# Neighbourhood attention by bands of 8 columns: a change to layer 0 of a four-layer hybrid kernel

## The chip, the core and the metric
The kernel runs on one core of a Trainium2 chip. The core has a matrix engine (PE in the profile, its weight loads PEld), a vector engine (DVE), a scalar engine that evaluates functions (ACT), a general one (POOL) and a queue that issues transfers (SP). Each engine executes its instructions in the order of the program; between engines there are semaphores. Data lie in an on-chip memory of 128 partitions, matrix products arrive in PSUM. The metric is the time of one execution in microseconds; less is better.

## The reference
Four layers run over an image tensor of shape (4, 56, 56, 128). The change touches layer 0 alone, attention of each pixel over a 7 x 7 neighbourhood, with 4 heads of 32 channels and a bias that depends on the relative position:
```python
qkv = (x @ w_qkv + b_qkv).reshape(B_, H_, W_, 3, nh, hd)
si = jnp.clip(jnp.arange(H_) - nb, 0, H_ - k)      # k = 7, nb = 3
sj = jnp.clip(jnp.arange(W_) - nb, 0, W_ - k)
...
attn = jnp.einsum('bnijd,bnipjqd->bnijpq', q, k_win) + bias[None]
attn = softmax over the 49 keys of a window
out = jnp.einsum('bnijpq,bnipjqd->bnijd', attn, v_win)
...
x = x + _L0_conv_ref(_gn(x), ...)                  # _gn: group norm over the image
```
At the border the window is shifted inwards, so that it always has 49 keys. Layers 1 to 3 (a selective scan, two attentions, two mixtures of experts) follow on the result.

## The kernel before
**Tiling.** An image has 3136 pixels. A *chunk* is 8 rows of 56 pixels (`SEQ` = 8, `CH` = 448), 7 chunks an image, 28 in all. Queries are columns of a matrix product, keys are its partitions. A *tile of keys* is 2 whole rows, 112 keys. A chunk's 8 query rows need 14 rows of keys, so up to 8 such tiles; each tile is met by the query rows whose windows touch it. `key_tiles` packs these (tile, query rows) pairs into *units* of exactly 448 query columns: 4 units a chunk, 112 in all, most of two pairs. Every unit computes all 112 x 448 scores, those outside a pixel's window too; these are later multiplied by zero.

**One unit.** `scores(i)` (L486): for each pair and head a matmul of 32 channels x 112 keys against the query columns; the four heads lie in the four row groups of the array and write to four PSUM banks. There are two such pairs of banks for halves of a unit, so the next unit's scores wait for the exps of this one. `weights(i)`: two exps on ACT (L496), then a product with exp(bias) (L502), three heads on DVE, one on POOL. `sums(i)` (L517): for each pair and head a matmul with the values (tile `o`) and one with ones (tile `d`, the denominator).

**One chunk.** `queries`, `keys`, `values` (L449, L457, L464) project the normed image; `finish` has four steps: `copied` (ACT takes `o` and `d` out of PSUM, POOL adds a bias into X, L533), `divided` twice (DVE: reciprocal L537 and product L538 on halves), `projected` (PE L543 and a DVE addition into X, L546). All small products of this kind and the transposes share a PSUM tile `m` with two buffers.

**Order.** The order on PE, ACT, DVE and POOL is written out by hand. In turn i of the main loop come the scores of unit i+1, the sums of unit i-1, the weights of unit i+1, and then the steps listed in `at[i]`: with four units a chunk, the queries of chunk k+1 at the first turn of chunk k, keys and values of chunk k+2 at the second and third, the steps of `finish` at turns 0 to 3 of the next chunk, 12 steps of the next image's norm one every one and a half turns (seven of them transpose a chunk, take its statistics on DVE and copy it on ACT), and 42 small steps that form layer 1's weights on DVE, one every second turn.

**Tables.** exp(bias) depends on the row offset, the key's column and the query's column. `make()` in `bias_tables` multiplies the bias by a constant table of 14 x 56 x 56, takes exps, writes them to DRAM (`dtab`, 7 transfers, L303) and reads them back into tables for inner rows and both edges (16 transfers, L311 and L318).

Of the kernel before, what the change touches and what calls it, by code (L numbers as in the profile page):

```python
# [10 lines left out]
F32 = mybir.dt.float32  # L11
AF = mybir.ActivationFunctionType
ALU = mybir.AluOpType
# [19 lines left out]
NEG = -1.0e30  # L33

# [32 lines left out]
def host_constants():  # L67

    j = np.arange(HW)
    start = np.clip(j - NB, 0, HW - KW)  # L70
    kj = j[:, None]
    inside = (kj >= start[None, :]) & (kj < start[None, :] + KW)
    toep = np.zeros((1 + KR, HW, HW), np.float32)
    toep[KR] = np.where(inside, 0.0, NEG)
    for d in range(KR):
        toep[d] = inside & (kj - j[None, :] + KW - 1 == d)
    turn = np.zeros((NH, KR, KR, NH), np.float32)
    for h in range(NH):
        for r in range(KR):
            turn[h, r, KR - 1 - r, h] = 1.0  # L80
# [24 lines left out]
    for i in range(B):  # L105
# [8 lines left out]
        "k_toep": toep.reshape(1 + KR, HW * HW),  # L114
        "k_turn": turn.reshape(NH * KR, KR * NH),
# [6 lines left out]
class Hybrid:  # L122
# [61 lines left out]
    def group_norm(self, b, pool, group):  # L184
# [11 lines left out]

        def turn(c, psum):
            g.ps = psum()
            for k in range(TC):
                nc.tensor.transpose(  # L200
                    g.ps[:, k * TP : (k + 1) * TP], self.X[b][:, TC * c + k, :],
                    self.ident[:TP, :TP],
                )
# [61 lines left out]
        g.place, g.turn, g.stats, g.raw = place, turn, stats, raw  # L265
        g.groups, g.normed, g.scaled = groups, normed, scaled
# [5 lines left out]
    def bias_tables(self, pool, tmp, big, dr, m):  # L272

        nc, a = self.nc, self.a
        inner = self.t(pool, [TP, 9, NH, HW], "e_inner")
        edge = [self.t(pool, [TP, 4, NB, NH, HW], f"e_edge{k}") for k in range(2)]
        nc.gpsimd.memset(inner, 0.0)
        for e in edge:  # L280
            nc.gpsimd.memset(e, 0.0)
        rpb = self.load(tmp, [NH * KR, KR], "rpb", a["L0_conv_rpb"].rearrange("h r d -> (h r) d"))
        order = self.load(tmp, [NH * KR, KR * NH], "rpb_turn", a["k_turn"])
        toep = self.t(big, [P, HW, HW], "xnT").rearrange("p k j -> p (k j)")[: 1 + KR]
        nc.sync.dma_start(out=toep, in_=a["k_toep"])
        rT = self.t(tmp, [1 + KR, KR * NH], "rpbT")
        nc.vector.memset(rT, 1.0)

        def make():

            ps = m()
            nc.tensor.matmul(ps[:KR, : KR * NH], rpb, order, start=True, stop=True)
            nc.vector.tensor_copy(rT[:KR], ps[:KR, : KR * NH])
            dtab = dr.tile([HW, KR, NH, HW], F32, name="dtab")
            rows = CH // HW
            for c in range(NCH):
                tab = self.t(tmp, [KR * NH, CH], "tab", bufs=4)
                ps = m()[: KR * NH]
                nc.tensor.matmul(
                    ps[:, :CH], rT, toep[:, c * CH : (c + 1) * CH], start=True, stop=True  # L300
                )
                nc.scalar.activation(tab, ps[:, :CH], AF.Exp)
                nc.sync.dma_start(  # L303
                    out=dtab[c * rows : (c + 1) * rows].rearrange("k r h j -> (r h) k j"),
                    in_=tab.rearrange("p (k j) -> p k j", j=HW),
                )
            for at, (q0, r0) in enumerate(((0, 0), (HW - NB, HW - KW))):
                for r in range(r0, r0 + KW):
                    t, r2 = r // 2, r % 2
                    first = KW - 1 - r + q0  # L310
                    nc.sync.dma_start(  # L311
                        out=edge[at][r2 * HW : (r2 + 1) * HW, t - r0 // 2],
                        in_=dtab[:, first : first + NB],
                    )
                if at:
                    continue
                for r2 in range(2):
                    nc.sync.dma_start(  # L318
                        out=inner[r2 * HW : (r2 + 1) * HW, 1 + r2 : 1 + r2 + KW],
                        in_=dtab[:, NB : NB + KW],  # L320
                    )

        return (inner, edge), make

    @staticmethod
    def window(i):
        return min(max(i - NB, 0), HW - KW)

    def key_tiles(self, c):


        rows = range(SEQ * c, SEQ * (c + 1))
        parts = []
        for t in range(NT):
            mine = [i for i in rows if self.window(i) <= 2 * t + 1 and self.window(i) + KW > 2 * t]
            if mine:
                parts.append((t, mine[0] - rows[0], mine[-1] + 1 - rows[0]))
        parts.sort(key=lambda x: x[1] - x[2])
        groups = []
        for p in parts:  # L340
            n = p[2] - p[1]
            for g in groups:

                if all(x[2] <= p[1] or p[2] <= x[1] for x in g):
                    g.append(p)
                    break
            else:
                groups.append([p])
        once = lambda g: sorted(i for _, q0, q1 in g for i in range(q0, q1)) == list(range(SEQ))
        return sorted(groups, key=lambda g: not once(g))  # L350

    def bias_slices(self, tables, c, part):

        inner, edge = tables
        t, q0, q1 = part
        out = []
        i = q0
        while i < q1:
            row = SEQ * c + i
            end = NB if row < NB else HW - NB if row < HW - NB else HW  # L360
            n = min(q1, end - SEQ * c) - i
            if row < NB:
                tab = edge[0][:, t, row : row + n]
            elif row >= HW - NB:
                tab = edge[1][:, t - (HW - KW) // 2, row - (HW - NB) : row - (HW - NB) + n]
            else:
                k = row - 2 * t + NB + 1
                tab = inner[:, k : k + n]
            out.append((i - q0, n, tab))
            i += n  # L370
        return out

    def layer0(self, wp1):
# [5 lines left out]
        with ExitStack() as ctx:  # L379
            wp = ctx.enter_context(tc.tile_pool(name="l0_w", bufs=1))  # L380
            dr = ctx.enter_context(tc.tile_pool(name="b_dram", bufs=1, space=DRAM))
# [9 lines left out]
            tables, make_tables = self.bias_tables(wp, wp, big, dr, m)  # L391
# [6 lines left out]
            make_tables()  # L398
# [11 lines left out]
            groups = {c: self.key_tiles(c) for c in range(NCH)}  # L410
            units = [(k, g) for k, (b, c) in enumerate(chunks) for g in range(len(groups[c]))]
            xn, q, kT, v, sc, es, out = {}, {}, {}, {}, {}, {}, {}

            def norm_steps(b):
                g = self.group_norm(b, big, group)

                def chunk(c):
                    if c == 0:
                        g.place(big)
                    g.turn(c, m)  # L420
                    g.stats(c)
                    g.raw(c)

                def hand_over():
                    g.normed(range(4, NCH))
                    xn[b] = g.xn.rearrange("p i j -> p (i j)")
# [16 lines left out]
            def chunk_of(k):  # L443
                b, c = chunks[k]
                return xn[b][:, c * CH : (c + 1) * CH]

            def queries(k):
                ps = m()
                nc.tensor.matmul(ps[:, :CH], wqkv[:, 0:C], chunk_of(k), start=True, stop=True)  # L449
                q[k] = self.t(sm, [P, CH], "q")  # L450
                nc.vector.tensor_scalar(
                    q[k], ps[:, :CH], bqkv[:, 0:1], HD**-0.5, op0=ALU.add, op1=ALU.mult
                )

            def keys(k):
                ps = m()
                nc.tensor.matmul(ps[:, :CH], wqkv[:, C : 2 * C], chunk_of(k), start=True, stop=True)  # L457
                kT[k] = self.t(sm, [P, CH], "k", bufs=5)
                nc.scalar.activation(kT[k], ps[:, :CH], AF.Identity, bias=bqkv[:, 1:2])

            def values(k):
                ps = m().rearrange("p (k c) -> p k c", c=C)
                for i in range(TC):
                    nc.tensor.matmul(  # L464
                        ps[:TP, i, :], chunk_of(k)[:, i * TP : (i + 1) * TP], wqkv[:, 2 * C :],
                        start=True, stop=True,
                    )
                v[k] = self.t(sm, [TP, TC, C], "v", bufs=5)
                nc.scalar.copy(v[k], ps[:TP])

            def parts(i):

                k, g = units[i]
                got, at = [], 0
                for t, q0, q1 in groups[chunks[k][1]][g]:
                    got.append((k - chunks[k][1] + t // TC, t % TC, at, (t, q0, q1)))
                    at += (q1 - q0) * HW
                return got, at

            def scores(i):  # L480
                k = units[i][0]
                sc[i] = [self.t(ps_s, [P, 2, 512], "s") for _ in range(2)]
                for kk, t, at, (_, q0, q1) in parts(i)[0]:
                    for h in range(NH):
                        own = slice(h * HD, (h + 1) * HD)
                        nc.tensor.matmul(  # L486
                            sc[i][h // 2][:TP, h % 2, at : at + (q1 - q0) * HW],
# [1646 lines left out]
```

## Time and profile before

| | us |
|---|---|
| runs, median (lowest to highest of 3) | 7244.53 (7239.55 to 7250.94) |
| the profiled execution: its time | 7253.18 |
| the profiled execution: span from first to last instruction | 7250.9 |
| layer 0, first scores to layer 1's first matmul | 35.4 to 576 |

The mean granted clock of the matrix engine is 0.928. The page's busy times over the whole span (PE 86%, DVE 82%, ACT 68%, POOL 42%) are an average over four layers; layer 0 is 8% of it. A busy PE in the records is not PE at its peak, as matmuls are pipelined and their ends are modelled; where it matters, distances from start to start are read. An fp32 matmul appears as two instructions, so 16 matmul records of scores are two parts of four heads. In groups by line, the columns are busy time and mean duration, then the idle time of the engine before them and what ended it.

### The profile page before, as it was taken

What the parts mean: (1) busy time and instruction counts of PE and PEld (TensorE: products, weight loads), DVE (VectorE), ACT (ScalarE), POOL (GpSimd) and SP (SyncE); (2) the same over time, 40 slices, a digit from 0 to 9 for tenths busy, and PEclk for the clock granted to TensorE, in tenths of its full rate; (3) what the DMA queues carried; (4) which work ended last, traced back from release to release, by engine and by line L of the source; (5) the groups of instructions that cost most, each with busy time, mean ns of one, the idle gap of its engine ahead of it and who ended that gap; (6) DMA issues with size and microseconds to landing.
All of it is one profiled execution on the core that took longest, in us unless ns stands there. A gap on an engine that the chain in (4) does not pass through costs nothing.

```text
span 7250.9 us, 101980 instructions
## 1 busy us (share of the span) xinstructions
PE 6239.1 (86%) x37329; PEld 2638.3 (36%) x37329; DVE 5938.2 (82%) x10315; ACT 4902.5 (68%) x4865; POOL 3012.2 (42%) x2106
## 2 busy tenths in 40 slices
PE   8888999999999999977777777777788889999998
PEld 4453233333333233332223322332333355555554
DVE  6886999999999999987788888888888753466665
ACT  4455776776776676758998999899899943322231
POOL 4556998999899899951001000000101200000000
PEclk9897998999899899978998999899999989999999
DMA  3005776777677677730000000000002304344433
GB/s 69 4 3 122 186 185 165 187 187 176 169 191 184 166 185 183 189 97 4 2 3 6 5 3 3 5 8 1 6 5 84 120 11 133 87 108 97 106 91 91
DMA packets 367267, 657.82 MB, mean 91 GB/s; under 512 B 98319, under 2 KB 214815, under 8 KB 366240
## 3 DMA queue, kind: packets, MB, share of 16 engines
q1 hardware_dynamic: 363597, 649.69, 35.8%
q8 instruction: 295, 4.83, 0.3%
q10 hardware_dynamic: 3168, 1.61, 0.1%
q14 instruction: 207, 1.69, 0.1%
HBM read 539.72 MB, written 105.02 MB: 89 GB/s over the span
## 4 chain that ended last, share of the span: by engine, by line
PE 22%; ACT 12%; DVE 11%; issue 8%; POOL 1%; SPq 0%; DMA 0%; DVEq 0%; ACTq 0%; POOLq 0%
ACT th L1236 9%; PE o L1874 6%; DVE th L1227 6%; PE q L1862 5%; PE s L1250 4%; PE pe L2069 2%; DVE X L2074 2%; ACT e L1264 1%; PE o L1280 1%; POOL e L1271 1%; PE m L1408 1%; DVE wide L1894 1%; PE m L1183 1%; DVE X L1416 0%; PE m L1691 0%
## 5 line engine op out<-in xcount | busy, mean ns | idle before, releaser
L1236 ACT ACTIVATE th<-th 128x5488 f32<-128x5488 f32 (+13 forms) x560 | 2184.5, 3944 | 187.6 <-DVE th L1227 162.2
L1227 DVE TENSOR_SCALAR th<-fT,g 128x784 f32<-128x784 f32 (+13 forms) x3920 | 1868.7, 549 | 310.1 <-PE s L1250 282.9
L817 POOL TENSOR_TENSOR hs<-hs,bc 128x896 f32<-128x896 f32 x896 | 1855.8, 2091 | 120.7 <-DVE hs L812 116.4
L1250 PE MATMUL s<-th,place 128*32 128x392 f32 (+5 forms) x14112 | 1396.5, 490 | 443.0 <-ACT th L1236 440.2
L812 DVE TENSOR_TENSOR_SCAN hs<-E,u 128x896 f32<-128x896 f32 x728 | 1448.9, 2006 | 1.8 <-ACT E L796 1.8
L796 ACT ACTIVATE E<-E,rate 128x448 f32<-128x448 f32 x1456 | 885.7, 661 | 124.5 <-DMA E<-delta_dram 120.7
L758 PE MATMUL u<-du,pick 32*128 32x448 f32 x2912 | 816.7, 629 | 140.7 <-DVE hs L812 137.6
L1250 PEld LDWEIGHTS s<-th,place 128*32 128x32 f32 (+1 forms) x14112 | 456.3, 112 | 1318.2 <-ACT th L1236 665.5
L805 DVE TENSOR_TENSOR u<-u,bc 128x896 f32<-128x896 f32 x728 | 783.3, 1076 | 67.5 <-PE u L758 67.3
L1867 ACT ACTIVATE e<-q,shift 128x448 f32<-128x448 f32 (+1 forms) x511 | 322.5, 634 | 673.1 <-PE q L1862 653.1
L1271 POOL TENSOR_TENSOR e<-e,later 112x112 f32<-112x112 f32 x112 | 155.0, 1384 | 1143.4 <-ACT e L1264 687.1
L2074 DVE SCALAR_TENSOR_TENSOR X<-pe,r_gate,X 112x128 f32<-112x128 f32 x896 | 311.8, 348 | 313.8 <-PE pe L2069 277.6
L823 PE MATMUL y<-hs,sum 128*32 128x448 f32 x3584 | 501.6, 633 | 4.0 <-POOL hs L817 4.0
L1862 PE MATMUL q<-xT 128*128 128x448 f32 (+1 forms) x1022 | 501.0, 573 | 0.9 <-ACT e L1867 0.9
L1874 PE MATMUL o<-e,xk 128*128 128x448 f32 (+1 forms) x1022 | 479.7, 553 | 16.3 <-ACT oT L1839 16.3
L1280 PE MATMUL o<-e,xk 112*128 112x392 f32 (+5 forms) x1024 | 393.6, 504 | 91.8 <-POOL e L1271 88.3
L1167 POOL MEMSET xa<- 112x4 f32 (+1 forms) x32 | 55.2, 1724 | 972.0 <-PE m L1160 971.9
L758 PEld LDWEIGHTS u<-du,pick 32*128 32x128 f32 x2912 | 246.2, 196 | 574.7 <-DVE hs L812 221.7
L2003 POOL MEMSET lc_xa<- 112x4 f32 x28 | 3.1, 110 | 949.1 <-DVE lc_xa L1997 700.2
L805 POOL TENSOR_TENSOR V<-V,bc 128x896 f32<-128x896 f32 x168 | 350.3, 2085 | 12.0 <-PE u L758 12.0
L800 ACT ACTIVATE u<-u 128x896 f32<-128x896 f32 x168 | 151.9, 904 | 295.8 <-PE u L749 215.9
L812 DVE TENSOR_TENSOR_SCAN hs<-u,V 128x896 f32<-128x896 f32 x168 | 338.1, 2013 | 0.0
(272 smaller groups left out, 8416.1 us busy)
## 6 DMA issues: line engine op xcount, KB each, us to landing
E<-delta_dram SPq DMA_DIRECT2D x728, 448.0 KB
V<-du_dram SPq DMA_DIRECT2D x168, 448.0 KB
wide<-in_L_ffn_weight SPq DMA_DIRECT2D x64, 1024.0 KB
r<-M SPq DMA_DIRECT2D x189, 224.0 KB
M<-wide SPq DMA_DIRECT2D x72, 392.0 KB
du_dram<-du SPq DMA_DIRECT2D x224, 112.0 KB
delta_dram<-delta SPq DMA_DIRECT2D x224, 112.0 KB
M<-wide SPq DMA_DIRECT2D x72, 168.0 KB
```

The source lines that it names most:

```text
L758: nc.tensor.matmul(halves(to)[:, k], w["pick"][own, q, :], pre[j]["du"][own, f], start=True, stop=True,)
L796: nc.scalar.activation(e, e, AF.Exp, scale=rate)
L805: eng.tensor_mul(v, v, pre[p // PAIRS]["bc"][:, 0:1].to_broadcast([P, 2, CH]))
L812: nc.vector.tensor_tensor_scan(flat, E.pop(p), V.pop(p), 0.0, op0=ALU.mult, op1=ALU.add)
L817: nc.gpsimd.tensor_mul(HS[p], HS[p], bc[:, 1:2].to_broadcast([P, 2, CH]))
L823: nc.tensor.matmul(py[j, f][r * HD : (r + 1) * HD, :], w["sum"][:, q, :], HS[p + r // 2][:, r % 2], start=False, stop=(q == QG - 1),)
L1227: nc.vector.tensor_scalar(th[i][:, s, lo:hi], fT[j][:, lo:hi], g[b, J // WT][:, at : at + 1], None, op0=ALU.add,)
L1236: nc.scalar.activation(own, own, AF.Tanh)
L1250: nc.tensor.matmul(ps[j, J][QW * blk : QW * blk + rows, h, lo:hi], place[:, off : off + rows], z[:, at + s, h * HALF + lo : h * HALF + hi] ...
L1280: nc.tensor.matmul(po[j][:, h, lo:hi], xk[b, J // WT][:, J % WT, :], e[:, h * HALF + lo : h * HALF + hi], start=(J == 0), stop=(J == t + ( ...
L1862: nc.tensor.matmul(ps[:n, :CH], of_tile(xT[b], t), xT[b][:, c * CH : (c + 1) * CH], start=True, stop=True,)
L1874: nc.tensor.matmul(po[b, c], xk[b][:n, t, :], e[:n], start=first, stop=last)
```

## The change
*Bands.* A tile of keys is now 8 columns by 14 rows (`BW`, `ROWS`), again 112 keys: the rows are those of a chunk's whole window, so all 8 query rows of a chunk meet the tile. The seven bands are met by 13, 14, 16, 14, 16, 14 and 11 query columns. `PARTS` puts bands 0, 2, 4, 6 into a unit that covers each of the 56 query columns once (448 query pixels) and bands 1, 3, 5 into one of 42 (336). A chunk has 2 units, 56 in all.

*Layout.* The normed image and the keys are stored as band, row, column in band; the keys of an image are one tile `kT` instead of a tile per chunk. Queries are written row by row; matmuls read and write them in pieces of 8 or 11 to 16 elements. The values of the 14 rows and 7 bands that a chunk needs are computed for each chunk in two halves (bands 0 to 3, 4 to 6); two adjacent chunks share rows, so these are 7 matmuls a chunk instead of 4.

*Tables.* Three tables (first, inner, last chunk) of 112 x 4 x 8 x 98 are formed on chip by 24 steps: each is 4 matmuls (one a head) of the bias rows spread over 112 partitions with a constant of 98 columns, and one exp, whose bias argument puts keys outside the window's rows to zero. Eight steps come before the first image's norm, two after each of its first eight steps. The DRAM round trip is gone. Each unit's products are then two instructions (DVE three heads, POOL one) instead of two to six.

*Order.* The turn is as before; the steps are listed anew for two turns a chunk. `d` has one buffer instead of two.
```diff
+PARTS = (
+    ((0, 0, 13), (2, 13, 29), (4, 29, 45), (6, 45, 56)),
+    ((1, 5, 19), (3, 21, 35), (5, 37, 51)),
+)
...
+        def raw_bands(c):
+            nc.scalar.copy(
+                g.xn[:, :, c * SEQ : (c + 1) * SEQ, :].rearrange("p b s j -> p s b j"),
+                g.ps[:, :CH].rearrange("p (s b j) -> p s b j", b=BANDS, j=BW),
+            )
...
+        def table(kind, i):
+            ps = m()[:TP, : NH * N].rearrange("p (h n) -> p h n", h=NH)
+            at = SEQ - 1 - i + (2 - kind) * NB
+            for h in range(NH):
                 nc.tensor.matmul(
+                    ps[:, h, :], r["rows"][:, h, at : at + ROWS, :].rearrange("p r k -> p (r k)"), cols,
+                    start=True, stop=True,
+                )
+            nc.scalar.activation(
+                tables[kind][:, :, i, :], ps, AF.Exp, bias=kill[:, kind * SEQ + i : kind * SEQ + i + 1]
+            )
...
+            kT = self.t(wp, [P, BANDS, HW, BW], "kT")
...
+            def values(k, half):
+                b, c = chunks[k]
+                own = range(0, 4) if half == 0 else range(4, BANDS)
                 ps = m().rearrange("p (k c) -> p k c", c=C)
+                for i, band in enumerate(own):
                     nc.tensor.matmul(
                         ps[:TP, i, :],
+                        xn[b][:, band, top(c) : top(c) + ROWS, :].rearrange("p r j -> p (r j)"),
+                        wqkv[:, 2 * C :], start=True, stop=True,
                     )
...
             def scores(i):
+                k, g = units[i]
+                t = top(chunks[k][1])
                 sc[i] = [self.t(ps_s, [P, 2, 512], "s") for _ in range(2)]
+                for band, j0, j1, at in parts(i):
                     for h in range(NH):
                         own = slice(h * HD, (h + 1) * HD)
+                        to = sc[i][h // 2][:TP, h % 2, : SEQ * WIDTHS[g]]
                         nc.tensor.matmul(
+                            by_row(to, WIDTHS[g])[:, :, at : at + j1 - j0],
+                            kT[own, band, t : t + ROWS, :].rearrange("p r j -> p (r j)"),
+                            by_row(q[k][own, :])[:, :, j0:j1], start=True, stop=True,
                         )
...
-                    r["o"], r["d"] = self.t(sm, [P, CH], "oT"), self.t(sm, [P, CH], "d")
+                    r["o"], r["d"] = self.t(sm, [P, CH], "oT"), self.t(sm, [P, CH], "d", bufs=1)
...
+            spread()
+            for i in range(SEQ):
+                table(0, i)
+            for n, step in enumerate(norm_steps(0)):
                 step()
+                for i in range(2 * n, min(2 * n + 2, 2 * SEQ)):
+                    table(1 + i // SEQ, i % SEQ)
...
                 if k + 1 < len(chunks):
                     add(i, queries, k + 1)
+                    add(i + 1, values, k + 1, 0)
+                    add(i + 2, values, k + 1, 1)
                 if k + 2 < len(chunks):
-                    add(i + 1, keys, k + 2)
-                    add(i + 2, values, k + 2)
+                    add(i, keys, k + 2)
                 end = first.get(k + 1, len(units))
-                for n, step in enumerate(finish(k)):
+                for n, step in zip((0, 1, 1, 2), finish(k)):
                     add(end + n, step)
                 if c == 0:
                     for n, step in enumerate(norm_steps(b + 1) if b + 1 < B else next_norm()):
-                        add(i + 3 * n // 2, step)
+                        add(i + 4 * n // 5, step)
             for n, step in enumerate(next_weights):
-                add(first[2] + 2 * n, step)
+                add(first[2] + n * 50 // len(next_weights), step)
```

## Prediction
> **What bounds the kernel now.** I read the clock and span first, then the busy time by stage, then layer 0 chunk by chunk, then one chunk in order of time, and last the waits. Busy time by stage (columns: window in us, its length, busy us of PE, PEld, DVE, ACT and POOL with instructions, clock, DMA share, GB/s):
> ```profile
> 0.00:36.00 36.00, 25.30 (x80) 12.21 (x80) 11.46 (x33) 12.83 (x22) 6.98 (x9) 1.00 0.84 187
> 36.00:576.00 540.00, 465.67 (x5661) 259.35 (x5655) 434.04 (x544) 269.98 (x369) 277.86 (x269) 0.92 0.07 13
> 576.00:2830.00 2254.00, 2072.77 (x8492) 688.77 (x8493) 2146.91 (x1476) 1558.74 (x2358) 2087.89 (x1183) 0.90 0.73 178
> ```
> The diff touches only the first two stages, 576 of 7250.9 us. In the second PE is busy 86% and DVE 80%; DMA stands still. In the third (layer 1) DVE is busy 95% on work that the diff leaves alone, so what layer 0 gains or loses reaches the end one for one. The ends of the stage in the timeline:
> ```profile
> 35.38 1.02 PE L486 MATMUL s<-q,k 32*112 32x448 f32 x8
> ...
> 575.18 1.19 PE L543 MATMUL m<-wproj,oT 128*112 128x128 f32 x4 [0.63 <-DVE oT L538]
> ...
> 576.17 4.41 PE L949 MATMUL m<-xnT,in_w 128*128 128x448 f32 x8
> ```
> The first scores start at 35.4, the last projection is followed at once by layer 1: 540.6 us for 28 chunks. The starts of L533, one for each chunk, give the length of each: with the next image's norm in it some 22.5, without 16:
> ```profile
> 62.90:85.10 22.20, 17.65 (x229) 10.08 (x221) 15.36 (x18) 11.89 (x18) 10.31 (x11) 1.00 0.89 153
> 85.10:108.00 22.90, 16.98 (x190) 10.31 (x188) 16.40 (x22) 8.22 (x12) 11.45 (x11) 0.85 0.04 8
> 128.10:144.10 16.00, 14.04 (x179) 8.19 (x178) 13.90 (x17) 7.37 (x10) 8.92 (x10) 0.89 0.01 1
> 144.10:160.70 16.60, 15.28 (x208) 8.10 (x208) 14.09 (x16) 9.25 (x13) 8.59 (x10) 1.00 0.01 2
> ```
> A quiet chunk is PE's (14.0 to 15.3 busy); a norm chunk loses 6 us more to a wait. One unit and that wait, in order of time:
> ```profile
> 206.83 1.07 PE L486 MATMUL s<-q,k 32*112 32x392 f32 x16
> ...
> 207.84 0.68 PE L517 MATMUL o<-e,v 112*32 112x280 f32 x8
> ...
> 208.33 0.66 PE L517 MATMUL d<-e,ones 112*32 112x280 f32 x8
> ...
> 208.80 0.47 PE L517 MATMUL o<-e,v 112*32 112x168 f32 x8
> ...
> 209.09 0.47 PE L517 MATMUL d<-e,ones 112*32 112x168 f32 x8
> ...
> 211.10 0.53 ACT L213 COPY xnT<-m 128x448 f32<-128x448 f32 x1 [5.66 <-DVE gn_st L210]
> ```
> Scores of 448 columns take 1.01 us start to start. Sums take 0.49 for 2 x 280 columns and 0.29 for 2 x 168: 0.87 ns a column and pass, whatever the length. ACT stood 5.66 us before its copy for the norm, because the statistics wait on DVE behind the reciprocals.
>
> **What the Trainium skill says.** "TensorE: Matmul & The Clock Gate", Part 3: matmuls in different row groups run together, and a weight load overlaps them where the row group differs. The trace agrees: 16 score matmuls in 1.07 us. "SBUF — State Buffer", Who interferes with whom: a DVE instruction with two SBUF inputs and a GpSimd one that reads SBUF exclude each other, and the loser blocks. It agrees: L502's 168-element form on DVE has a mean of 836 ns, where the 1176-element one has 1386. The first TensorE page, Part 1, puts the idle array at half clock; the trace agrees, though its clock column says 1.00: the first transposes' eight weight loads take 1.41 us, later four take 0.39.
>
> **The change, part by part.**
> *Fewer columns.* A chunk had 4 units of 448 query columns, now it has 448 + 336 = 784 instead of 1792, in 7 bands instead of 8 parts. PE per chunk, at full clock: scores 1.01 + 0.76; sums 784 x 2 outputs x 2 passes x 0.87 ns = 2.7, and 0.3 for the many starts; queries and keys 0.9 each (201.20 to 202.15); values 14 x 0.116 = 1.6 (8 took 0.93); projection 1.0; a transposed chunk 0.5. Sum 9.7, at clock 0.92 10.6, against 15.0 by the same rows before.
> DVE per chunk: bias 1344 and 1008 elements at 1.2 ns (L805: 896 in 1076) = 1.6 + 1.2; reciprocals 2 x 1.54 and products 2 x 0.53 = 4.1; X 0.68; queries 0.67; statistics 0.62; normed 0.50; the next layer's weights 0.9. Sum 10.3, against 15. ACT: exps 1.73 + 1.4, copies and keys 3.4: 6.5. POOL: 1.05 + 0.8 + 1.3 (at 2.33 ns an element, L817): never the bound.
>
> *Tighter steps.* Two loop turns per chunk instead of four make a ring. The queries of chunk k+1 are now computed in the turn just before the scores that read them (before: four turns ahead), and their PSUM tile m is the one (of two) that the projection before held until DVE's addition into X. DVE is strictly in order, so from the end of one even unit's exps to the next one's: bias 1.6, both divisions 4.1, bias of the odd unit 1.2, addition 0.7, PE queries 0.9 and keys 0.9 (DVE's q lies beside them), scores 1.0, exps 1.73; six hand-overs of 0.12 (ACT ends 202.77, DVE starts 202.88) 0.7; some 0.3 of gaps on DVE. Sum 13.1 us per chunk. It is over PE's 10.6 and DVE's 10.3, so the ring binds: 28 x 13.1 = 367. Behind the waiting queries stand, on PE, keys, scores and all of the next turn.
> *Norm and weight steps.* They now fall in 9 turns of 14, not 18 of 28. In odd turns the statistics queue behind both divisions and ACT's raw copy holds up the next exps: 2 us each, twice. Two transposes in turns 0 and 4: 1.1 and 2.1. Turn 2: 0.8; the group steps, with DVE, PE and ACT in series (0.16-us pieces, a sqrt between), 1.6 and 1.9; normed 1.0 and 2.4. Together 15 us an image (now 17: 22.2 + 22.9 + 20.1 less 3 x 16). Three images and 8 for layer 1's first norm: 53. Half of the 42 weight steps (0.55 to 0.72) stand in the ring: 10.
> *Waits I cost at nothing.* One kT tile for an image, written in rows beside those being read: if the scores also waited for the keys' copy just made, +0.9 a chunk, 25 in all. I take 0, since waits follow the regions used: here the sums of a unit's first part start before its second part is multiplied.
> ```profile
> 560.07 0.67 DVE L502 TENSOR_TENSOR e<-e,e_inner 112x168 f32<-112x168 f32 x1
> ...
> 560.64 0.84 PE L517 MATMUL o<-e,v 112*32 112x392 f32 x8
> ```
> The d buffer, now single: its divisions end a turn before the next copy. SP loses 23 table transfers (7, 14 and 2) and two loads and gets three small ones; its last waits before were for taps, and the last weight step, turn 52 of 56, is still ahead of layer 1. Weights of 32x112 for 112 columns instead of up to 448: if they no longer hide (59 ns each when 16 take 0.94), scores take 1.9 + 1.4 and the ring grows by 0.9: 0 to 25 us, I take 0. Short runs (8, 11 to 16 elements) in matmul reads and PSUM writes: no row shows them; 0 to a doubled rate, I take 0.
> *Tables.* 24 tables of 4 heads, each 8 matmul passes of 98 columns: 0.7 us warm, 1.35 cold, and an exp of 392 (0.55). Loads and the spread end near 5 us; eight tables to 12.7; seven norm steps with two tables each, the transposed tile held through statistics and raw copy, 2.55 each, to 30.6; then what took 10.9 before (24.5 to 35.4) and 1.3 for the last two tables. First scores at 43 instead of 35.4. If PE stays cold, 52.
> *Sum.* 43 + 367 + 53 + 10, and 10 for the last chunk's copies, divisions and projection: 483 instead of 576, so -93. The profiled execution took 7253.18 (span 7250.9), which gives 7160; the median of the runs is 7244.53, 8.7 lower, so 7151.
>
> **The rivals.**
> - Ring binds (forecast): 7151, own range 7125 to 7180. For it: queries just ahead of use, PSUM pairs, 4.1 us of divisions in one turn. Against: every hand-over was read from other pairs.
> - PE binds, the ring being looser than I read it (tiles come free earlier): 10.6 and 0.4 of hand-overs that stay make 11.0 a chunk, and the weight steps hide: 43 + 308 + 53 + 10 = 414, -162: 7083. For it: the quiet chunks before are PE's. Against: the ring is longer by 2.
> - The ring plus a cover that is gone: the keys' copy, or bare weight loads, or POOL winning the shared port before DVE (1.05 per unit): +1.5 a chunk, 42 us: 7193. For it: the 836 ns of small forms. Against: the started-early sums above.
> - Slower than before: short runs cost PE its rate. Queries, scores and sums stream 4.7 us a chunk; PE's 10.6 must reach (576 - 116) / 28 = 16.4 before the stage is as long as now, an extra 5.8, so each such column must cost 2.15 times. At 2.5 times: 10.6 + 7.0 / 0.92 = 18.2, 28 x 18.2 + 116 = 626: 7295. Against: rows of 56 in 59 (L949) stream a pass of 448 columns in 0.38 us, 0.85 ns each, as contiguous ones do.
>
> **How the numbers follow.** 0.55 for the ring, 0.20 for PE, 0.21 for the lost cover, 0.04 for slower. Predicted 7151. The range takes in PE's case and the lost cover with a small margin: 7075 to 7203. Under 0.2% (14.5 us) a measurement can't tell a change from none. Faster 0.94, same 0.02, slower 0.04.
>
> **What would show it.** Sums and scores at 0.87 ns a column and pass, else short runs matter. First scores at 43. Quiet chunks of 13.1 with PE busy near 10; 11 says PE, 14.5 a lost cover. PE standing before the queries for DVE's addition into X, and before the scores for DVE's q or ACT's keys. Layer 1's 2254 us unchanged. The prediction is wrong if quiet chunks lie under 12 or over 14, or the start over 50.

## The result and the profile after

Medians of four runs each, taken side by side: 7151.16 us after (7144.59 to 7156.75), 7247.73 before (7239.55 to 7251.57). The ratio is 0.987, 95% interval 0.985 to 0.989: 96.6 us less. The profiled span is 7155.0 instead of 7250.9, the mean clock 0.927 instead of 0.928.

Busy time by stage after, with stages cut at the first scores and at layer 1's first matmul (columns as before):
```profile
0.00:45.00 45.00, 35.78 (x259) 29.66 (x263) 12.41 (x37) 23.06 (x39) 1.47 (x7) 0.92 0.72 131
45.00:491.00 446.00, 337.18 (x5544) 255.63 (x5538) 273.58 (x361) 178.55 (x285) 139.92 (x85) 0.86 0.05 10
491.00:2745.00 2254.00, 2069.47 (x8497) 688.10 (x8500) 2147.96 (x1476) 1559.24 (x2359) 2088.98 (x1184) 0.91 0.73 178
```
In the second stage no engine is near its limit any more: PE is busy 76% (was 86%), DVE 61% (was 80%), and the granted clock fell from 0.92 to 0.86. Something else sets the pace. Layer 1 has the busy times it had. The ends of the stage in the timeline of after:
```profile
44.66 0.80 PE L485 MATMUL s<-q,kT 32*112 32x104 f32 x20
...
489.89 1.20 PE L542 MATMUL m<-wproj,oT 128*112 128x128 f32 x4 [1.14 <-DVE oT L537]
...
490.88 0.95 PE L955 MATMUL m<-xnT,in_w 128*128 128x448 f32 x1
```
446.2 us for 28 chunks, 540.8 before. Windows of after from one POOL addition (L532) to the next: the first two carry the next image's norm, the third doesn't but is the last chunk of an image, the fourth is a common quiet chunk:
```profile
155.40:176.10 20.70, 14.84 (x221) 11.03 (x221) 13.52 (x19) 8.29 (x15) 5.52 (x4) 0.91 0.01 2
176.10:193.10 17.00, 12.29 (x197) 9.12 (x197) 9.07 (x12) 5.17 (x8) 5.48 (x4) 0.80 0.00 1
245.10:257.30 12.20, 9.67 (x194) 7.55 (x194) 8.26 (x10) 5.65 (x9) 4.65 (x4) 1.00 0.01 1
370.20:384.90 14.70, 11.37 (x195) 8.07 (x194) 8.44 (x11) 5.65 (x9) 4.55 (x5) 0.88 0.01 3
```
In the third window PE has 9.67 us of work at clock 1.00, the forecast's 9.7. In the fourth the same work takes 11.37 us, partly at half clock, and PE stands still for 3.3. The same chunk in order of time, from the projection's first half to the next exps:
```profile
369.52 0.69 PE L542 MATMUL m<-wproj,oT 128*112 128x128 f32 x4 [0.49 <-DVE oT L537]
371.75 0.69 PE L542 MATMUL m<-wproj,oT 128*112 128x128 f32 x4 [1.53 <-DVE oT L537]
...
372.94 0.68 DVE L545 TENSOR_TENSOR X<-m,X 112x512 f32<-112x512 f32 x1
...
373.67 1.86 PE L434 MATMUL m<-xnT,wqkv 128*128 128x448 f32 x2 [0.58 <-DVE X L545]
...
375.32 1.70 PE L446 MATMUL m<-xnT,wqkv 128*128 128x448 f32 x2
...
377.06 0.63 ACT L450 ACTIVATE kT<-m,bqkv 128x448 f32<-128x448 f32 x1 [2.59 <-PE m L446]
...
377.75 1.09 PE L485 MATMUL s<-q,kT 32*112 32x104 f32 x32 [0.72 <-ACT kT L450]
378.93 1.73 ACT L497 ACTIVATE e<-s 112x896 f32<-112x896 f32 x2 [1.24 <-PE s L485]
```
Read it as the forecast ring. PE's queries wait for DVE's addition (0.58); they and the keys then run for 1.86 and 1.70 us, where the warm passes before took 0.9 each. The scores don't start with q: they start 0.06 us after ACT's copy of the keys ends. The waits from 60 to 480 us say that this is the rule (columns: sum in us, times, longest), first lines left out:
```profile
DVE q L439 <- PE m L434: 35.1, 23, 2.6
PEld s L485 <- ACT kT L450: 33.1, 19, 2.1
PE s L485 <- ACT kT L450: 13.8, 19, 0.7
PEld m L434 <- DVE X L545: 12.8, 12, 1.9
```
One unit of sums, later in the same timeline:
```profile
446.50 0.38 PE L515 MATMUL d<-e,ones 112*32 112x112 f32 x8
...
446.69 0.38 PE L515 MATMUL o<-e,v 112*32 112x112 f32 x8
...
446.88 0.37 PE L515 MATMUL d<-e,ones 112*32 112x112 f32 x8
...
447.08 0.37 PE L515 MATMUL o<-e,v 112*32 112x112 f32 x8
```
They start 0.193 us apart on average: 112 columns and two passes, 0.86 ns each, where the kernel before had 0.87 with whole rows. The runs of 14 elements cost nothing.

### The profile page after: what moved, and what is told of

Read it like the earlier page. It is cut to its first block, busy times and chain, and to the rows that moved or that the text cites. A ratio compares the mean times of both kernels' runs of the same rounds, so it can differ in the third digit from the quotient of the medians.

```text
span 7155.0 us, 101398 instructions
## 1 busy us (share of the span) xinstructions
PE 6103.2 (85%) x37386; PEld 2646.8 (37%) x37386; DVE 5779.6 (81%) x10135; ACT 4820.8 (67%) x4798; POOL 2868.5 (40%) x1920
## 4 chain that ended last, share of the span: by engine, by line
PE 22%; ACT 12%; DVE 11%; issue 9%; POOL 1%; SPq 0%; DMA 0%; DVEq 0%; ACTq 0%; POOLq 0%
ACT th L1242 9%; PE o L1880 6%; DVE th L1233 5%; PE q L1868 5%; PE s L1256 4%; PE pe L2075 2%; DVE X L2080 2%; ACT e L1270 1%; POOL e L1277 1%; PE o L1286 1%; PE m L1414 1%; PE m L1189 1%; DVE wide L1900 1%; DVE X L1422 0%; PE m L1697 0%
```

## The experiments

The theory after the result: a *ring* through queries, keys and the keys' copy sets layer 0, and the half clock lengthens it. The rivals: the array alone is too slow (half clock), the divisions are what is too long, or the norm's stalls. Lengths are from the first scores to layer 1's first matmul, in the profiled execution; the ratio is to the kernel before, run beside it.

| kernel | median us | ratio (95%) | first scores | layer 0 | layers 1 to 3 | clock from 60 us to near layer 0's end |
|---|---|---|---|---|---|---|
| before | 7247.73 | | 35.4 | 540.8 | 6674.8 | 0.93 |
| after | 7151.16 | 0.987 (0.985 to 0.989) | 44.7 | 446.2 | 6664.1 | 0.86 |
| e1 keys early | 7152.05 | 0.987 (0.986 to 0.989) | 45.4 | 442.4 | 6669.1 | 0.84 |
| e2 queries early | 7143.5 | 0.986 (0.985 to 0.988) | 44.9 | 434.9 | 6660.4 | 0.89 |
| e3 both early | 7102.42 | 0.980 (0.979 to 0.982) | 44.0 | 394.1 | 6662.2 | 0.89 |
| e4 after, again | 7149.83 | 0.987 (0.986 to 0.989) | 45.0 | 443.1 | 6658.0 | 0.87 |
| e5 warm array | 7147.15 | 0.986 (0.984 to 0.987) | 43.8 | 436.9 | 6665.1 | 0.94 |
| e7 norm first | 7173.23 | 0.989 (0.988 to 0.991) | 45.7 | 462.8 | 6661.6 | 0.86 |
| e8 both early, norm first | 7085.58 | 0.977 (0.975 to 0.979) | 45.4 | 381.2 | 6662.1 | 0.92 |
| e9 divisions apart | 7160.78 | 0.988 (0.986 to 0.990) | 45.8 | 442.9 | 6668.1 | 0.86 |
| e10 all, divisions apart | 7134.27 | 0.984 (0.983 to 0.986) | 44.0 | 425.6 | 6661.7 | 0.88 |
| e11 before, again | 7249.92 | 1.000 (0.999 to 1.001) | 35.6 | 541.7 | 6668.0 | 0.93 |

### e1, e2, e3: keys and queries a turn earlier

Each alone (e1 the second line, e2 the first), then both (e3):
```diff
-                    add(i, queries, k + 1)
+                    add(max(i - 1, 0), queries, k + 1)
...
-                    add(i, keys, k + 2)
+                    add(max(i - 1, 0), keys, k + 2)
```


> Keys of chunk k+2 one turn earlier, queries left where they are. Ring theory (the chunk's length is the round trip through DVE's addition into X, the queries, the keys' copy on ACT, the scores and the exps): the scores then start at DVE's q instead of at ACT's copy of the keys, so quiet chunks go from 14.2 to 13.2 us and layer 0 gets shorter by 20 to 35 us. PE-bound theory (the same matmuls in another order): no change, within 5 us. Waits-follow-regions theory in its first form (the keys' copy is not waited for): no change either.

> Queries of chunk k+1 one turn earlier, keys left. Ring theory: the scores still wait for the keys' copy, which now follows DVE's addition directly (the keys take the PSUM tile that the projection held), so only the 0.9 to 1.8 us of the queries' matmul leave the ring: quiet chunks 13.0, layer 0 shorter by 25 to 40 us. PE-bound theory: no change within 5 us.

> Both one turn earlier. Ring theory: addition, queries, q and keys leave the ring; what stays is bias, divisions, projection, second values, scores and exps, about 11.5 to 12 us a quiet chunk, layer 0 shorter by 50 to 70 us, and PE nearly its bound. PE-bound theory: no change within 5 us. If DVE is the bound (10.3 us of work a chunk) and the waits are only its shadow: no change either.

e1 brought 1 to 4 us and e2 8 to 11, both less than expected; both together 49 to 52. The waits of e1 from 60 to 480 us show why it alone is worth so little:
```profile
PEld s L485 <- DVE q L439: 28.0, 15, 2.1
...
PE s L485 <- DVE q L439: 19.0, 23, 1.2
```
The wait for the keys' copy is gone, and the same instruction now waits for q, the queries being still the last thing before it, and still in part at half clock (24 of their 56 passes take over 0.8 us, 32 in after). In e2 it is the other way round:
```profile
PEld s L485 <- ACT kT L450: 32.3, 19, 2.1
...
PE s L485 <- ACT kT L450: 14.9, 19, 1.1
```
Two waits lie side by side in the ring, and only with both taken out does it open. Two quiet chunks of e3, in windows:
```profile
121.60:131.60 10.00, 9.95 (x196) 7.49 (x196) 8.98 (x10) 5.54 (x9) 4.66 (x5) 1.00 0.01 2
131.60:141.50 9.90, 9.85 (x195) 7.42 (x195) 9.07 (x11) 5.55 (x9) 4.55 (x4) 1.00 0.02 3
```
PE is busy without a break and its clock is 1.00: in these chunks the forecast's second case, PE as the bound, is reached by moving two steps. It also shows that the ring held PE back, not the reverse. The whole of layer 0 isn't at that bound: an image's seven chunks still take 99 us between the POOL additions, 29 over 7 x 9.9, and four chunks, in the stretch of the next image's norm steps, take all of the excess (20.3, 19.3, 15.8 and 14.1 us, from 141.5 us on). In e1 there was one more effect, which the expectation left out: the product after a division (L537) has a mean of 634 ns instead of 499 in after, and of 390 when undisturbed. Of its 56 executions 14 are long; each of these ends 0.25 us after an instruction of POOL does, 10 of them after POOL's addition into X (L532), beside which the longest, 1.47 us, ran from its start.

### e4: the changed kernel again

> The changed kernel once more, to tell layer 0 from the rest. If the 10 us that the trace shows gained after layer 0 are an effect of the change, this trace's layers 1 to 3 take 6664 us again (from layer 1's first matmul to the end), as against 6675 in the kernel before. If they are the spread of one code between executions, it lies anywhere within about 10 us of these, and layer 0 is again 490.9 us long within 2.

It repeats within 3 us in layer 0 and differs by 6 in layers 1 to 3. Layer 0 was expected to end within 2 us of 490.9 and ended at 488.1. So differences of 3 us in layer 0, e1's among them, aren't told from none.

### e5: a warm array

Three more products of 384 columns ahead of each projection, into the same tile, which the projection then overwrites:
```diff
-                    ps = m().rearrange("p (k c) -> p k c", c=C)
+                    ps = m()
+                    for _ in range(3):
+                        nc.tensor.matmul(ps[:, : 3 * C], wqkv[:, 0:C], wqkv, start=True, stop=True)
+                    ps = ps.rearrange("p (k c) -> p k c", c=C)
```


> The changed kernel with three extra matmuls of 384 columns ahead of each projection, into the PSUM tile that the projection then overwrites; nothing reads them. They are 1.9 us of PE work a chunk at full clock, in the gap in which PE waits for the divisions. Clock theory (the gaps let the array fall to half clock, so that queries, keys and scores run slowly on the ring): the mean clock of layer 0 rises from 0.86 to over 0.93, the passes of queries and keys from 0.80 us towards 0.5, and layer 0 gets shorter by 15 to 30 us in spite of the added work. If the clock is granted by something other than idle gaps, or PE's work is the bound: layer 0 longer by 0 to 50 us (28 x 1.9).

The window from 60 to 480 us of e5, and the wait for the keys' copy there:
```profile
60.00:480.00 420.00, 350.88 (x5480) 259.84 (x5479) 265.33 (x353) 168.54 (x271) 130.63 (x82) 0.94 0.02 4
```
```profile
PE s L485 <- ACT kT L450: 13.8, 19, 0.7
```
The clock rose to 0.94 and the passes of queries and keys over 0.8 us fell from 60 of 112 (47 in e4) to 20. Layer 0 became 6 to 9 us shorter, though PE was given more to do: the half clock is a part of the ring. It is less than the 15 to 30 expected. The wait for the copy is the same 13.8 us as in after. The gain lies in the twelve quiet chunks (without norm steps), from one even unit's exps to the next: they have a mean of 13.2 us, against 14.2 in after and 14.1 in e4, some 11 us in all, while the other chunks got 1 to 4 us longer together. So the half clock is worth about 1 us of a quiet chunk, with what the added products cost the ring already taken off.

### e7, e8: the norm's steps ahead of the others in their turn

```diff
-                    for n, step in enumerate(norm_steps(b + 1) if b + 1 < B else next_norm()):
-                        add(i + 4 * n // 5, step)
+                    steps = norm_steps(b + 1) if b + 1 < B else next_norm()
+                    for n, step in reversed(list(enumerate(steps))):
+                        at.setdefault(i + 4 * n // 5, []).insert(0, step)
```
e7 is this on the changed kernel, e8 on e3.

> The changed kernel with each turn's norm step ahead of the turn's other steps, so that in odd turns the statistics go before both divisions on DVE. My account of the norm (2 us lost in each odd turn with a transposed chunk, three images and the next layer's first norm, plus m tiles held): layer 0 shorter by 10 to 20 us, all of it in chunks with a norm, and ACT's wait of 5.9 us before its raw copy gone. If the norm's cost is its own work: no change.

> Queries and keys a turn earlier and the norm steps first. With the ring open, the norm's stall is what is late next: run e3 loses 29 us an image in its norm chunks over seven quiet ones of 9.9. If the stall is the statistics behind the divisions: layer 0 shorter than in e3 by 20 to 45 us, so 350 to 375 us from first scores to layer 1. If not: as e3, 394.

e7 went the wrong way by 17 to 20 us. Lines of its timeline, an odd turn and then an even one:
```profile
173.63 0.53 ACT L222 COPY xnT<-m 128x448 f32<-128x448 f32 x1 [2.17 <-DVE gn_st L240]
...
180.97 1.62 PE L460 MATMUL m<-wqkv,xnT 128*112 128x128 f32 x6 [1.83 <-ACT xnT L222]
...
198.00 2.05 PE L542 MATMUL m<-wproj,oT 128*112 128x128 f32 x8 [5.20 <-ACT xnT L222]
```
In odd turns ACT's wait for the statistics fell from up to 6.0 us to 2.17, as meant. In even turns the transpose now takes one of the two `m` tiles before the values, and PE stands until the raw copy gives it back, 1.83 us here. Where two chunks are transposed in one turn, both tiles are taken, and the projection waits, 5.20 us in the last line. That is the larger part: from 60 to 480 us PE waited 23.8 us for the raw copy before projections, 9.4 in after. Inside the closed ring that is lost at once. With the ring open (e8) the same edit gains 13 us, less than the 20 to 45 expected. e8 is the best kernel of this study, 0.977 (0.975 to 0.979) of before; its quiet chunks stay at PE's 9.9.

### e9, e10: the two divisions in separate turns

```diff
-                for n, step in zip((0, 1, 1, 2), finish(k)):
+                for n, step in zip((0, 1, 2, 3), finish(k)):
```
e9 is this on the changed kernel, e10 on e8. A first form, e6, also had two buffers of `d`. It has no time, as it doesn't fit on the chip: a pool that needs 4.875 kB of each partition finds 3.53 left.

> The changed kernel with the second half's division one turn later and the projection of the sums two turns later; nothing is left out. If the 4.1 us of both divisions, which stand in one turn ahead of the odd bias, are what makes the ring long, halving them there leaves the ring shorter by up to 2 us a chunk where the other turn has room: layer 0 from its first scores to layer 1 at 390 to 430 us (443 to 446 in the changed kernel), median 7095 to 7140. If the ring is closed by the queries and the keys at the head of each turn instead, every turn's DVE work only moves to the other turn: 440 to 450, median 7145 to 7160. A cost of its own: the copy of the next chunk's sums then waits on ACT for the second division of the chunk before, as the divisor has one buffer.

> Queries and keys a turn early, normalization ahead of the other steps, and the divisions one to a turn; nothing is left out. If after the ring is opened the array is the bound of layer 0 (quiet chunks 9.9 us with both early), moving a division changes nothing: layer 0 at 375 to 387 us (381 without the divisions apart), median 7080 to 7092, quiet chunks 9.9. If DVE's two divisions still delay the odd exponentials there, layer 0 at 340 to 370 and quiet chunks at 9 to 9.5. If the copy that waits for the divisor's one buffer holds ACT, 390 to 410.

e9 changed nothing in layer 0, and e10 lost 44 us against e8. Its layer 0 of 425.6 us lies above even the 390 to 410 that its expectation had as the worst case. Their waits name the cost that had been put at the end of both expectations, the first fence e9's (60 to 480 us), the second e10's (60 to 400 us):
```profile
PEld s L485 <- ACT kT L450: 68.5, 19, 7.6
ACT d L531 <- DVE oT L537: 64.8, 22, 6.4
```
```profile
PE d L515 <- ACT d L531: 45.3, 20, 5.4
ACT d L531 <- DVE oT L537: 38.8, 16, 5.3
```
ACT's copy of the next denominators waits for the second division of the chunk before, because `d` has one buffer, and behind it on ACT stands the keys' copy: in e9 that wait rose from 33.1 to 68.5 us. So the single buffer is free only where both divisions stand in one turn, as in the changed kernel. Whether two divisions in one turn cost anything where `d` has two buffers stays open, as e6 has no time.

### e11: the kernel before, again

> The kernel before, profiled once more; nothing is changed. If its layers 1 to 3 take about 6675 us again, the 10 us by which those of the changed kernel were shorter belong to the change; if they take 6658 to 6669 like those of the seven runs since, they are what one execution differs from another, and only layer 0 was changed. Layer 0 from its first scores to layer 1's first matmul at 538 to 543 in both cases.

Layers 1 to 3 took 6668.0, within the 6658.0 to 6669.1 of the ten other traces whose layers 1 to 3 are the same code; the first trace's 6674.8 is above them all. Followed instruction by instruction from layer 1's start, all these traces keep their distance from one another through layer 1 (-1.2 to 4.7 us against after) and drift apart by several us more in layer 2's attention, each in its own way.

## Why the prediction was right, and where it wasn't

The forecast 7151 met the median 7151.16. That it came so close is luck, for the errors have opposite signs. By a sign that the forecast set itself, quiet chunks under 12 or over 14 us, the length of its ring was wrong: they took 14.2, near the 14.5 that it gave for a lost cover, and one cost named in that rival, the keys' copy, is in fact on the path.

| term | forecast | measured in the trace |
|---|---|---|
| first scores | 43 | 44.7 |
| ring, 28 chunks, and half of the weight steps | 367 + 10 | 28 x 14.2 = 397 |
| norm | 53 | about 39 (446.2 less the 397 and a tail taken at 10) |
| layer 1's first matmul | 483 | 490.9 |
| layers 1 to 3, against the trace before | 0 | -10.7 |
| from the profiled execution to the median | -8.7 | -5.6 |

Two sums of the prediction come out otherwise when redone: 9.7 at clock 0.92 is 10.5, not 10.6, and half of 42 weight steps of 0.55 to 0.72 us is 12 to 15 us, not 10. Neither changes which case binds.

*The ring binds: right.* The forecast chain was in the trace step by step. In the quiet chunk shown, DVE's addition ends 7.63 us after the even exps, forecast 7.6. e3 confirms it: taking PE's queries and keys off the chain makes PE the bound of the quiet chunks.

*Its size, 13.1: the failed step is "if the scores also waited for the keys' copy just made ... I take 0, since waits follow the regions used".* The wait is there in most chunks. That waits follow regions is not refuted; the region was misread. The 8 query rows of chunk k+1 need 14 rows of keys, so their last rows belong to chunk k+2, whose keys are made in that same turn. It is a true dependence. The last chunk of an image has no further rows, and there the scores start with q (the window of 12.20 us). In the chunk shown it costs 0.7 us: from the keys' end at 377.02 to the scores at 377.75. The bound of 0.9 a chunk had the right size; the choice of its lower end was the error.

*Queries and keys at 0.9 each: mis-sized.* Together they take 3.35 us in the chunk shown (373.67 to 377.02), 1.5 more than forecast. The forecast had the half clock among its facts but gave it to PE's total only, at 0.92, not to the instructions that stand behind a wait, which are the ones that pay. The clock in this chunk, in stretches:
```profile
366.73:370.15 3.42, 2.93 (x78) 2.31 (x77) 3.39 (x4) 1.94 (x3) 2.61 (x2) 1.00 0.00 0
370.15:373.56 3.41, 1.41 (x11) 1.15 (x10) 3.38 (x5) 0.43 (x2) 1.29 (x2) 1.00 0.00 0
373.56:376.97 3.41, 3.30 (x4) 1.18 (x4) 0.94 (x3) 0.91 (x3) 0.00 (x0) 0.50 0.00 0
376.97:380.39 3.42, 2.70 (x97) 2.52 (x96) 0.00 (x0) 2.09 (x3) 0.00 (x0) 1.00 0.02 7
```
In layer 0 of this trace the granted clock changes only at the edges of such stretches of 3.41 us. In the second one PE is busy for 1.41 us, under half of it; the next has half clock, and the queries and keys fall into it. Of the 94 stretches of layer 0 with full clock, 21 are followed by half clock: in them PE is busy for 7 to 53% of the time, in the 73 others for 51% or more. In the twelve traces together a border at 52% puts all but 21 of 1226 such stretches on the right side. The chunk at 450 us was just above it (1.79 us of 3.40) and its queries ran warm, in 1.02 us. The Trainium skill, "TensorE: Matmul & The Clock Gate", Part 1, names such short idle pieces between groups of matmuls as a cause of falling back to half clock. It also gives an idle window of about 3.4 us for the fall. The trace agrees with the first and with the length of the window, but the window need not be idle throughout: before these queries PE stood 0.49, 1.53 and 0.58 us within 4.7 us, and in no piece near 3.4.

So 14.67 in that chunk is 13.1, and 0.7 and 1.5, less about 0.6 of hand-overs and gaps that were priced too high. The 12 quiet chunks have a mean of 14.2 from one even unit's exps to the next; with warm queries, but with the copy, one of them took 12.9, and in e5, with PE kept busy, their mean is 13.2.

*The tables: 43 against 44.7, right within 2.* In the timeline of after each pair of tables, with the norm step beside it, follows the pair before by 2.70 us, where 2.55 had been taken:
```profile
18.86 2.02 PE L346 MATMUL m<-cols,e 112*112 112x98 f32 x16 [0.29 <-ACT tab L350]
...
21.56 2.02 PE L346 MATMUL m<-cols,e 112*112 112x98 f32 x16 [0.29 <-ACT tab L350]
```

*The norm: 53 against about 39.* An image's seven chunks took 116.7 and 112.8 us between the POOL additions, so 17 and 13 over 7 x 14.2: the 15 an image were right. What is missing may lie in layer 1's norm or in overlap with a ring that already stood; as the term is a remainder, its parts aren't told apart. The term also depends on the ring: with the ring open (e3) an image loses 29 us, not 15.

*Costed at nothing and rightly so:* short runs (0.86 ns a column and pass, so the slower case falls), bare weight loads (32 records of scores in 1.09 us), the single `d` buffer (in this order; e9 shows its price in another). POOL running ahead of DVE, the third rival's last part, cost the division's products nothing over the forecast in the chunk shown: they took 0.39 and 0.72 us, forecast 2 x 0.53.

*"One for one": true through layer 1.* From its first matmul it took 2644.2 us until layer 2's first tanh, 2644.3 before. Beyond that the first two traces differ by 10.7, which the forecast didn't have and which more than made up for the 8 us by which layer 0 ended too late. e11 puts the trace before at the upper end of what one execution of the same code differs from another. Still, the medians lie 97 us apart and layer 1's start only 87 (576.2 and 577.4 against 490.9 and 488.1); what the other 10 are isn't settled, and the spread of single traces, 11 us, is as large.

## What to carry to other kernels

When a loop gets fewer turns, draw the ring anew: each step placed just before its reader puts its engine's wait, its hand-overs and its cold clock on the path, and two such steps side by side must both be moved before either is worth much (1 to 11 us alone here, 49 to 52 together). A "wait for a neighbouring region" is checked against what the reader's window spans, at its last row, before it is costed at nothing. And price an instruction that stands behind a wait at half clock where PE was busy for less than about half of the 3 to 4 us before it, even if the stage's mean clock looks high (0.92 before, 0.86 after).

## What the hardware showed that was not expected

- The half clock needed no long idle time: it followed stretches of 3.41 us in which PE was busy for less than about half, with gaps of 0.5 to 1.5 us, none longer, in the chunk shown. The queries then took 1.86 us instead of 1.02. With work put into the gaps (e5), layer 0's clock rose from 0.86 to 0.94, and its time fell.
- Matrix products that read and write runs of 14 elements stream as fast as whole rows: 0.86 ns a column and pass.
- One DVE product of 128 x 224 took 0.39 us alone and, in e1, up to 1.47 beside POOL's addition into X; each long one ended 0.25 us after a POOL instruction.
